# A decoder layer in fp32 on one core: value transposes one product later, and two empty steps a tile in the second batch's cross stage

## Chip, core and metric

One core of a Trainium2 chip runs the kernel. The metric is the device time of one execution in microseconds. The time before is the median of three runs.

## The reference

A decoder layer over two batches of 512 tokens with 1024 features. Three stages follow each other, each with a residual and a layer norm:

```python
x = _layernorm(x + attn(x, wq, wk, wv, wo))       # 32 query heads, 8 key/value heads of 128, causal window of 128
x = _layernorm(x + xattn(x, ctx))                 # round and clip x and ctx to 0..255, then one product 512x1024x1024 per batch
x = _layernorm(x + ffn(x, w_gate, w_up, w_down))  # 2752 inner features, silu(gate) * up, rounded to whole numbers
```

## The kernel before

TensorE (PE) does all products. Most of them are fp32 and go through Strassen's scheme (`strassen`, a generator): a pair of 128-row weight blocks times a 1024 x 512 right-hand matrix is done as seven products of four 128x128x256 matmuls, in the order 1, 6, 5, 2, 7, 4, 3, with sums on VectorE (DVE) and ScalarE (ACT) between them. Each product is one step of the generator (`yield`). The trace has two records for one fp32 matmul.

**Attention.** A group is one batch and one key/value head; there are 16. `pieces(m + 1)` yields the steps of the next group's projections while `scores` and `weigh` do the current group. `project` makes three Strassen runs for a group: j = 0 gives kT and vT, j = 1 and 2 give the queries. After the first run `transpose_v` turns vT into v by four PE transposes (tile `vtr`, L308), an ACT copy (L310) and a DVE difference `vd` (L312). A tile of 128 tokens has six calls of `other`, each of which takes one step of `pieces` and one step of work lent by `between`. The transposed probabilities `pt` (L374), the transposed values `vtr` and the weighted sums `o` (L395 to L398) all use the pool `ps_t`, which has one buffer.

**Output projection** (tiles `y`, L563, with left factors `ol` and right ones `or`, `ot`) runs as lent work behind the attention of batch 1 and the feed-forward of batch 0.

**Cross stage.** `Cross.tokens` handles the four tiles of a batch in the order 2, 3, 0, 1, so that tile 1 (t = 5 in the second batch) is the last. For each it yields steps: layer norm of x (two), quantise (DVE), `whole` (ACT, gives a1), eight PE transposes `q` (L679) with the ACT copy to a1T (L680), two halves of `m` (L686, eight bf16 matmuls each, read by DVE in L687 and L688), a second layer norm (L77 to L85, two steps), and eight transposes of x (L695) with ACT copies into x2T (L696).

**Feed-forward.** A unit is 128 gate and 128 up features of one batch: seven products with the right-hand matrix x2T (L132), `activate` (the ACT and DVE steps L786 to L798, giving `act`), and a part of the down product `d` (L818), which is done for two units at a time in batch 0. Batch 0 has 21 full units and a rest unit (`rest`, L810) of 64 + 64 features, then batch 1 follows. `load_down` loads the down weights, `split` and `rest_of_split` make their hi and lo parts (L767, L774). The products, `q`, `m`, the transposes of x and `rest` take PSUM buffers from one pool of two, `ps_p`; some products have a second pool.

**What sets the order.** The second batch's cross stage is lent work of batch 0's feed-forward. `in_feed_forward` is called once after each of the seven products of a unit, and the queue `aside` is

```python
aside.add(iter([None] * 28))
aside.add(cross.context(1), 2)
aside.add(cross_tokens(1), 2)
```

where the 2 means that a step is taken in every second call. Before the rest unit of batch 0, `finish_between()` issues all that is left in the queues. Then the right-hand differences of x2T[1] (L102) are made, which batch 1's products need. A scheduler below the kernel reorders independent instructions within each engine, taking the order of the source as the priority; tiles of a pool are given out in source order.

Of the kernel before, what the change touches and what calls it, by code (L numbers as in the profile page):

```python
# [118 lines left out]
def strassen(nc, spaces, work, left, right, outs, name, sums=None):  # L119

    c11, c12, c21, c22 = outs

    def like(y):
        return y if len(c11.shape) == 2 else y.rearrange("p (k c) -> p k c", c=c11.shape[2])

    def product(ps, k, start):  # L130
        for c in range(KH):
            nc.tensor.matmul(ps, left[k - 1][:, c, :], right[k - 1][:, c, :],  # L132
                             start=start and c == 0, stop=c == KH - 1, skip_group_check=True)

    def bank(k):
        return spaces[k // 2].tile([P, NH], F32, tag="p", name=f"prod{k}_{name}")

    if sums is None:
        sums = [work.tile([P, NH], F32, tag=f"st{k}", name=f"st{k}_{name}", bufs=1) for k in range(3)]
    p1, u2, u3 = sums  # L140
    one, two = bank(0), bank(1)
    product(one, 1, True)
    nc.scalar.copy(p1, one)
    yield
    product(two, 6, True)
    nc.vector.tensor_tensor(u2, two, p1, ALU.add)
    yield
    roomy = spaces[0] is not spaces[1]
    if roomy:
        three = bank(2)  # L150
        product(three, 5, True)
        yield
    product(one, 2, False)
    nc.scalar.copy(c11, like(one))  # L154
    yield
    product(two, 7, False)
    nc.vector.tensor_tensor(u3, two, p1, ALU.add)  # L157
    yield
    if roomy:
        nc.vector.tensor_tensor(c22, like(three), like(u3), ALU.add)  # L160
        four = bank(3)
        product(four, 4, True)
        nc.vector.tensor_tensor(c21, like(four), like(u3), ALU.add)
        yield
    else:
        three = bank(2)
        product(three, 5, True)
        nc.vector.tensor_tensor(c22, like(three), like(u3), ALU.add)
        yield
        product(two, 4, False)  # L170
        nc.vector.tensor_tensor(c21, like(two), like(p1), ALU.add)
        yield
    product(three, 3, False)
    nc.vector.tensor_tensor(c12, like(three), like(u2), ALU.add)
    yield
# [33 lines left out]
def attention(nc, tc, consts, xbuf, tpool, wpool, ps_p, ps_y, dram, kept, complete, between):  # L209
# [7 lines left out]
    with ExitStack() as ctx:  # L217
# [11 lines left out]
        PAIRS = 1 + G // 2  # L229
# [3 lines left out]
        def load_weight(n):  # L233
            if n >= len(order):
                return
            _, g, j = order[n]
            w = wpool.tile([P, 2, KC, P], F32, tag="w", name=f"w_{n}")
            for h in range(2):
                src = (wv_d if h else wk_d)[g] if j == 0 else wq_d[g * G + 2 * (j - 1) + h]
                nc.sync.dma_start(out=w[:, h], in_=src)  # L240
            weights[n] = w

        def prepare(n):
            if n < len(order):
                lefts[n] = strassen_left(nc, tc, wpool, weights[n], f"s_{n}")
# [20 lines left out]
        def project_first(outs):  # L266

            ps = [ps_p.tile([P, N], F32, tag="p", name=f"first{h}") for h in range(2)]
            for c in range(KC):

                for k, part in enumerate((ts(0, NH), ts(1, NH)) if c == 0 else (slice(None),)):
                    for h in range(2):
                        nc.tensor.matmul(  # L273
                            ps[h][:, part], weights[0][:, h, c], x0[:, c, part],
                            start=c == 0 and k == 0, stop=c == KC - 1, skip_group_check=True,
                        )
            for h in range(2):
                nc.scalar.copy(outs[h], ps[h])
            load_weight(2)
            prepare(1)  # L280
            right[0] = strassen_right(nc, tpool, x0, "t_0")

        def project(n):

            b, g, j = order[n]
            if j == 0:
                c1 = kT[b, g] = kvpool.tile([P, N], F32, tag="kT", name=f"kT_{n}")
                c2 = vT[b, g] = kvpool.tile([P, N], F32, tag="vT", name=f"vT_{n}", bufs=1)
            else:
                if j == 1:  # L290
                    qT[b, g] = qpool.tile([P, N // BLOCK, G, BLOCK], F32, tag="qT", name=f"qT_{b}_{g}")
                c1, c2 = (qT[b, g][:, :, 2 * j - 2 + h] for h in range(2))
            if n == 0:
                project_first((c1, c2))
                yield
                return
            outs = [c[:, ts(half, c.shape[1] // 2)] for c in (c1, c2) for half in range(2)]
            for k, _ in enumerate(strassen(nc, (ps_p, ps_y if b == 0 else ps_p), work, lefts.pop(n), right[b], outs, n)):
                if k == 4:
                    prepare(n + 1)  # L300
                elif k == 6:
                    load_weight(n + 2)
                yield LUMP if k == 4 else None

        def transpose_v(b, g):
            ps = ps_t.tile([P, TPB, P], F32, tag="t", name=f"vtr_{b}_{g}")
            for i in range(TPB):
                nc.tensor.transpose(ps[:, i, :], vT[b, g][:, ts(i, P)], ident)  # L308
            v[b, g] = kvpool.tile([P, TPB, P], F32, tag="v", name=f"v_{b}_{g}")
            nc.scalar.copy(v[b, g], ps)  # L310
            vd[b, g] = kvpool.tile([P, TPB - 1, P], F32, tag="vd", name=f"vd_{b}_{g}")
            nc.vector.tensor_tensor(vd[b, g], v[b, g][:, 1:], v[b, g][:, : TPB - 1], ALU.subtract)  # L312

        def pieces(m):

            b, g = groups[m]
            for j in range(PAIRS):
                yield from project(m * PAIRS + j)
                if j == 0:
                    transpose_v(b, g)  # L320
                    yield

        def scores(b, g, i, meanwhile):

# [106 lines left out]
        for _ in pieces(0):  # L431
            pass
# [150 lines left out]
class Cross:  # L583
# [74 lines left out]
    def tokens(self, b, x2T, complete):  # L658
        nc, a2, base = self.nc, self.a2[b], self.base[b]
        one, raw, work, ps_p = self.pools  # L660
        for i in (2, 3, 0, 1):
            while (b, i // 2) not in complete:
                yield
            t = b * TPB + i
            x = self.xres[t]
            yield from layer_norm(nc, work, x)
            yield
            tmp = raw.tile([P, D], F32, tag="raw", name=f"tmp_{t}")
            a1 = work.tile([P, D], BF16, tag="a1", name=f"a1_{t}", bufs=1)
            rows = work.tile([P, 1], F32, tag="rows", name=f"rows_{t}")  # L670
            self.quantise(x, 0, tmp)
            yield
            self.whole(a1, tmp, rows)
            yield
            nc.vector.tensor_tensor(rows, rows, self.c12[:, 1:2], ALU.mult)
            a1T = work.tile([P, KC, P], BF16, tag="a1T", name=f"a1T_{t}", bufs=1)
            ps = ps_p.tile([P, KC, P], BF16, tag="p", name=f"q_{t}")
            for c in range(KC):
                nc.tensor.transpose(ps[:, c, :], a1[:, ts(c, P)], self.ident_bf)  # L679
            nc.scalar.copy(a1T, ps)  # L680
            yield
            for e in range(2):
                half = ts(e, HALF)
                ps = ps_p.tile([P, HALF], F32, tag="p", name=f"m_{t}_{e}")
                for c in range(KC):
                    nc.tensor.matmul(ps, a1T[:, c, :], a2[c][:, half], start=c == 0, stop=c == KC - 1)  # L686
                nc.vector.scalar_tensor_tensor(tmp[:, half], ps, rows, base[:, half], ALU.add, ALU.add)  # L687
                nc.vector.scalar_tensor_tensor(x[:, half], tmp[:, half], self.s12, x[:, half], ALU.mult, ALU.add)  # L688
                yield
            yield from layer_norm(nc, work, x)  # L690
            yield
            for e in range(2):
                ps = ps_p.tile([P, KC // 2, P], F32, tag="p", name=f"x2_{t}_{e}")
                for c in range(KC // 2):
                    nc.tensor.transpose(ps[:, c, :], x[:, ts(e * (KC // 2) + c, P)], self.ident)  # L695
                nc.scalar.copy(x2T[:, ts(e, KC // 2), ts(i, P)], ps)  # L696
            if t in self.spill:
                nc.sync.dma_start(out=self.spill[t], in_=x)
            yield
# [524 lines left out]
```

## Time and profile before

| | |
|---|---|
| median of three runs | 1900.16 us (1898.99 to 1901.72) |
| profiled execution | 1899.1 us, span 1897.4 us |
| PE busy | 1870.3 us, 8666 records |
| DVE busy | 1370.6 us |
| ACT busy | 562.6 us |
| DMA | 416.88 MB, mean 220 GB/s |
| chain that ended last | PE 84%, DVE 10%, ACT 3%, DMA 2% |

PE, DVE and ACT are the matmul, vector and scalar engines, PEld is PE's weight load, SP issues DMAs. A row of the timeline has start (us), duration (us), engine, line, operation, out<-in and count; an idle time before it stands in brackets with what ended it. PE records overlap: one of 128x256 lasts 379 ns and the next starts 216 ns after it.

### The profile page before, as it was taken

To read this page: it belongs to the slowest core of one execution; us is meant where nothing else is said; L and a number is where in the kernel's file an instruction comes from. 1 tells how busy PE (TensorE), PEld (TensorE's weight loads), DVE (VectorE), ACT (ScalarE), POOL (GpSimd) and SP (SyncE) were. 2 spreads that over 40 slices of the span, in tenths; PEclk is the share of its full clock that TensorE was granted. 3 is DMA by queue.
4 is the path that set the end of the run, shared out by engine and by line. 5 is a ranking of instruction groups with operands and counts; after the bars stand their busy time and mean duration, and the time that the engine had idled before them with its cause. 6 is when DMAs were issued, how large, how long until landed. Compare 5 with 4: busy or idle time off the path is not lost.

```text
span 1897.4 us, 24656 instructions
## 1 busy us (share of the span) xinstructions
PE 1870.3 (99%) x8666; PEld 1548.1 (82%) x8678; DVE 1370.6 (72%) x3021; ACT 562.6 (30%) x1571; POOL 13.8 (1%) x32
## 2 busy tenths in 40 slices
PE   9999999999999999999999999999999999999997
PEld 6888888878888888888777888888788778888885
DVE  4678888787777676767787667767777697655657
ACT  1334433332211221233543111112233244321224
POOL 0000000000000000000000000000000000000000
PEclk9999999999999999999999999999999999999999
DMA  8478888777888888856368777766344244544431
GB/s 310 170 263 287 287 280 289 263 242 255 276 305 273 277 284 287 273 187 224 115 213 287 264 274 249 261 239 211 122 152 147 84 158 170 200 139 134 166 128 45
DMA packets 183323, 416.88 MB, mean 220 GB/s; under 512 B 16672, under 2 KB 93728, under 8 KB 183200
## 3 DMA queue, kind: packets, MB, share of 16 engines
q1 hardware_dynamic: 181760, 412.94, 63.5%
q10 hardware_dynamic: 1440, 2.36, 0.3%
q8 instruction: 69, 1.13, 0.2%
q14 instruction: 54, 0.44, 0.1%
HBM read 318.77 MB, written 96.47 MB: 219 GB/s over the span
## 4 chain that ended last, share of the span: by engine, by line
PE 84%; DVE 10%; ACT 3%; DMA 2%; issue 1%; SPq 0%; DVEq 0%; ACTq 0%
PE prod L132 49%; PE y L563 16%; PE d L818 7%; PE ps L338 3%; PE o L397 2%; PE o L398 2%; PE m L686 1%; PE pt L374 1%; DMA wd<-in_wd_dram 1%; PE first L273 1%; PE o L395 1%; ACT s L362 1%; DMA ol<-kept 1%; DVE factors L409 0%; DVE lo L774 0%
## 5 line engine op out<-in xcount | busy, mean ns | idle before, releaser
L563 PE MATMUL y<-or,ol 128*128 128x256 f32 x896 | 243.6, 379 | 1.3 <-DMA ol<-kept 1.2
L563 PEld LDWEIGHTS y<-or,ol 128*128 128x128 f32 x896 | 169.0, 190 | 28.0 <-issue 3.6
L563 PE MATMUL y<-ot,ol 128*128 128x256 f32 x672 | 184.3, 382 | 1.8 <-DVE ot L507 1.5
L132 PE MATMUL prod<-xT,w 128*128 128x256 f32 x752 | 182.7, 380 | 0.1
L132 PE MATMUL prod<-t,w 128*128 128x256 f32 x752 | 177.2, 379 | 0.0
L132 PE MATMUL prod<-t,s 128*128 128x256 f32 x752 | 176.7, 379 | 0.1
L132 PE MATMUL prod<-x2T,wgu 128*128 128x256 f32 x672 | 160.1, 380 | 0.2 <-DMA sgu<-sums 0.2
L132 PEld LDWEIGHTS prod<-t,w 128*128 128x128 f32 x752 | 140.1, 190 | 23.6 <-issue 6.7
L132 PE MATMUL prod<-t,wgu 128*128 128x256 f32 x672 | 159.4, 379 | 0.0
L132 PEld LDWEIGHTS prod<-xT,w 128*128 128x128 f32 x752 | 139.4, 190 | 24.3 <-issue 6.7
L132 PEld LDWEIGHTS prod<-t,s 128*128 128x128 f32 x752 | 140.3, 190 | 23.1 <-issue 4.8
L132 PE MATMUL prod<-t,sgu 128*128 128x256 f32 x672 | 155.7, 379 | 0.5 <-ACT g L154 0.5
L563 PEld LDWEIGHTS y<-ot,ol 128*128 128x128 f32 x672 | 124.8, 190 | 27.3 <-DVE ot L507 6.4
L132 PEld LDWEIGHTS prod<-x2T,wgu 128*128 128x128 f32 x672 | 127.3, 190 | 18.9 <-ACT g L154 0.6
L132 PEld LDWEIGHTS prod<-t,wgu 128*128 128x128 f32 x672 | 127.2, 190 | 18.9 <-issue 0.5
L132 PEld LDWEIGHTS prod<-t,sgu 128*128 128x128 f32 x672 | 127.2, 190 | 18.8 <-ACT g L154 0.9
L362 ACT ACTIVATE s<-s,top 128x128 f32<-128x128 f32 x256 | 99.6, 390 | 34.0 <-DVE top L359 33.2
L818 PE MATMUL d<-hi,act 128*128 128x512 f32 x256 | 108.6, 425 | 0.4 <-DVE act L798 0.2
L348 ACT COPY s<-ps 128x128 f32<-128x128 f32 x192 | 39.5, 232 | 228.1 <-PE ps L338 228.0
L832 DVE TENSOR_TENSOR acc<-d,acc 128x512 f32<-128x512 f32 x104 | 71.1, 690 | 43.5 <-PE d L818 43.1
L818 PE MATMUL d<-lo,act 128*128 128x512 f32 x256 | 101.1, 395 | 0.0
L157 DVE TENSOR_TENSOR st<-prod,st 128x256 f32<-128x256 f32 x89 | 37.5, 422 | 83.0 <-PE prod L132 82.7
(220 smaller groups left out, 2983.5 us busy)
## 6 DMA issues: line engine op xcount, KB each, us to landing
kept<-factors SPq DMA_DIRECT2D x112, 448.0 KB, 3.6
ol<-kept SPq DMA_DIRECT2D x112, 448.0 KB, 5.3
w<-in_wq_dram SPq DMA_DIRECT2D x64, 512.0 KB, 4.6
or<-wo_sums SPq DMA_DIRECT2D x64, 512.0 KB, 5.1
sgu<-sums SPq DMA_DIRECT2D x42, 768.0 KB, 6.4
or<-in_wo_dram SPq DMA_DIRECT2D x48, 512.0 KB, 4.6
wgu<-in_wgu_dram SPq DMA_DIRECT2D x42, 512.0 KB, 4.1
wd<-in_wd_dram SPq DMA_DIRECT2D x42, 512.0 KB, 3.5
```

Of the source, the lines that this page charges most:

```text
L132: nc.tensor.matmul(ps, left[k - 1][:, c, :], right[k - 1][:, c, :], start=start and c == 0, stop=c == KH - 1, skip_group_check=True)
L157: nc.vector.tensor_tensor(u3, two, p1, ALU.add)
L273: nc.tensor.matmul(ps[h][:, part], weights[0][:, h, c], x0[:, c, part], start=c == 0 and k == 0, stop=c == KC - 1, skip_group_check=True,)
L338: nc.tensor.matmul(ps[:, k, cut // BLOCK : G + 1].rearrange("p d w -> p (d w)"), qT[b, g][:, G * i + c].rearrange("p h w -> p (h w)"), kT[ ...
L348: nc.scalar.copy(s[:, c, c * BLOCK :], ps[:, k, : G - c].rearrange("p d w -> p (d w)"))
L362: nc.scalar.activation(s[:, h, :], s[:, h, :], AF.Exp, bias=top[:, h : h + 1], scale=QSCALE, accum_out=total[:, h : h + 1],)
L374: nc.tensor.transpose(ps[:, :, ts(c, BLOCK)], s[:, c, :], ident)
L397: nc.tensor.matmul(ps, v[b, g][:, i - 1, :], both, start=True, stop=False)
L398: nc.tensor.matmul(ps, vd[b, g][:, i - 1, :], cur, start=False, stop=True)
L563: nc.tensor.matmul(banks[bank][:, half], left[:, SLOT[j]], mine[j], start=grow[k][0] and g == 0 and half == 0, stop=g == LAST, skip_group_ ...
L818: nc.tensor.matmul(ps, act[:, ts(i, P)], half[:, part], start=start and k == 0, stop=stop and k == len(parts) - 1)
L832: nc.vector.tensor_tensor(acc[t][:, ts(e, HALF)], ps, acc[t][:, ts(e, HALF)], ALU.add)
```

## The change

In `pieces`, the transposes of a group's values are issued after the first product of the second Strassen run instead of before it. In `Cross.tokens`, for the second batch alone, a tile gets two steps in which nothing is issued: one after `whole`, and one after the copy to a1T.

```diff
@@ pieces
             for j in range(PAIRS):
-                yield from project(m * PAIRS + j)
-                if j == 0:
-                    transpose_v(b, g)
-                    yield
+                for k, lump in enumerate(project(m * PAIRS + j)):
+                    yield lump
+                    if j == 1 and k == 0:
+                        transpose_v(b, g)
+                        yield
@@ Cross.tokens
             self.whole(a1, tmp, rows)
             yield
+            if b:
+                yield
             nc.vector.tensor_tensor(rows, rows, self.c12[:, 1:2], ALU.mult)
...
             nc.scalar.copy(a1T, ps)
             yield
+            if b:
+                yield
             for e in range(2):
```

The line numbers of the profile before are those of the kernel before; in the changed kernel L308 to L312 stay, L374 is L375, L395 is L396, L679 is L682, L686 is L691, L695 is L700, and all that follows is five later.

## Prediction

> **What bounds the kernel now.** I read the page's shares first, then what PE itself waited for, then the timeline at the places that the edits touch. The page:
>
> ```profile
> PE 1870.3 (99%) x8666; PEld 1548.1 (82%) x8678; DVE 1370.6 (72%) x3021; ACT 562.6 (30%) x1571; POOL 13.8 (1%) x32
> ```
>
> PE works for 1870.3 of 1897.4 us. DVE is busy 72% and ACT 30%, so they set the end only where PE's next instruction needs something they have not finished. PE takes its instructions in one fixed order, so every stall of PE adds its full length. The built changed program holds the same number of instructions of every kind on PE, DVE and the DMA queues; ACT has two table loads fewer. What can move is the stalls alone. The list of what PE waited for (total us, times, longest us) has these three lines for the stages of the two edits:
>
> ```profile
> PE vtr L308 <- DVE vT L171: 1.3, 1, 1.3
> PE m L686 <- ACT a1T L680: 1.1, 1, 1.1
> PE m L686 <- DVE tmp L687: 1.0, 1, 1.0
> ```
>
> The whole prize is therefore 3.4 us: one wait of a value transposition, and two waits in second-batch tiles, at 1342.6 and 1388.6. The timeline at the second shows what such a wait is (start, us, engine, line):
>
> ```profile
> 1385.49 0.61 PE L679 MATMUL q<-ident_bf,a 128*128 128x128 bf16 x8
> 1385.94 1.51 PE L132 MATMUL prod<-t,wgu 128*128 128x256 f32 x6
> 1387.50 1.00 ACT L680 COPY a1T<-q 128x1024 bf16<-128x1024 bf16 x1
> 1388.56 1.90 PE L686 MATMUL m<-a,a1T 128*128 128x512 bf16 x7 [1.10 <-ACT a1T L680]
> ```
>
> Three instructions of a product (six records) stand between the transposes q and the matmul m, and ACT's copy of a1T ends later than they do.
>
> The last of the four tiles of the second batch, as it runs before the change:
>
> ```profile
> 1485.23 0.39 PE L679 MATMUL q<-ident_bf,a 128*128 128x128 bf16 x4
> ...
> 1493.28 1.89 PE L686 MATMUL m<-a,a1T 128*128 128x512 bf16 x7
> ...
> 1496.30 1.89 PE L686 MATMUL m<-a,a1T 128*128 128x512 bf16 x8
> ...
> 1498.23 0.75 DVE L687 SCALAR_TENSOR_TENSOR tmp<-m,rows,base 128x512 f32<-128x512 f32 x1 [0.22 <-PE m L686]
> ...
> 1500.02 0.68 DVE L77 BATCH_NORM_STATS2 ln_stats<-xres 128x6 f32<-128x512 f32 x1
> ...
> 1502.42 0.81 DVE L85 TENSOR_SCALAR xres<-xres,ln_mv,ln_r 128x1024 f32<-128x1024 f32 x1
> ...
> 1508.65 0.60 PE L695 MATMUL x<-ident,xres 128*128 128x128 f32 x4
> ```
>
> Between q, m and the transposes of x (L695) PE has 6.2 us and more of other products, so the whole chain q, a1T, m, layer norm costs nothing. The end of the first batch's units, after that tile:
>
> ```profile
> 1521.03 1.89 PE L132 MATMUL prod<-x2T,sgu 128*128 128x256 f32 x8
> 1522.75 6.17 PE L810 MATMUL rest<-x2T,wgu 128*128 128x512 f32 x14
> 1522.97 0.42 DVE L174 TENSOR_TENSOR g<-prod,st 128x256 f32<-128x256 f32 x1
> ...
> 1523.49 0.63 ACT L786 ACTIVATE sg<-g 128x512 f32<-128x512 f32 x1 [5.31 <-DVE g L174]
> ...
> 1528.76 1.89 PE L132 MATMUL prod<-x2T,wgu 128*128 128x256 f32 x8
> ```
>
> After unit 20's last product (ends at 1522.7) the activation of unit 20 is a chain of DVE and ACT steps, and PE meanwhile does the rest unit; no wait of PE stands in this stretch.
>
> **The change, part by part.** *The transposition of the values.* Steps eight and nine of a group trade places; the number of steps, the place of each loan of a step to other work, and every DMA issue stay. vtr now stands behind product 1 (eight records of 0.216 us spacing, 1.73 us: the prod rows above start 1.73 us apart for eight) and, in the built order, behind o instead of before it. The 1.3 us wait was for vT's last sum, queued on DVE behind sums of weights and kept factors (0.68 and 1.08 us each in the timeline at 404); 1.73 us covers it: -1.3. ACT's copy of v (0.585 us) and DVE's vd (0.55 us) come one product later; v and vd are for the next group, many products on. The single PSUM buffer that pt, o and vtr share is next asked for by the next tile's pt, several products behind, so 0 there; if that cover were gone it would be the 0.585 us copy, up to 15 times.
>
> *The empty steps, first three tiles.* In the built order 19, 48 and 14 PE instructions now stand between q and m of the first three tiles; 3 stood in the second one before, where the 1.1 us were lost: -1.1. The 1.0 us at 1342.6 is m's second half, which waits until DVE has read the first; DVE was at a 1.23 us split (L774). There the cover grows only from two instructions (0.86 us) to three (1.30 us). DVE's read is 0.2 + 0.75 us when DVE is free, so I take -1.0, and -0.4 if DVE is as late again.
>
> *The empty steps, last tile.* The cross stage's steps are called once in two products of the feed-forward, and the first batch has 21 units x 7 = 147 products. I counted the calls from the source: before, the four tiles start at calls 65, 85, 105, 125 and the last ends by call 147, exactly in time. With 12 steps a tile instead of 10 they start at 65, 89, 113, 137, and six of the last tile's twelve steps are left when the products end. finish_between then issues them all at once: second empty step, m, layer norm, x transposes. PE's order in the built program becomes: last product of unit 20, q x8, m x16, four d of unit 20, x transposes x8, rest, unit 22. Nothing else can be put between: rest (L810) takes its PSUM buffer from the same pool of two as q, m and the x transposes, after them; more d need act of the rest unit, or a bank that the first two hold; unit 22's products need x2T[1].
>
> I walk this by hand, with A = the end of unit 20's last product. q: A+0.45 (8 x 0.056). ACT stands with sg of unit 20 ahead of a1T: L174 A+0.2 to 0.62 (0.42; PE to DVE costs 0.2 in the rows above), sg to A+1.3 (0.63), a1T to A+2.25 (1.01, overlapping a little). m starts A+2.3: **stall 1.85**. m's sixteen end at A+5.75 (16 x 0.216). d needs act of unit 20. DVE's order there interleaves both chains: L787, L788, L789 (0.69, 0.69, 0.42) to A+3.2; ACT mag 0.63 to A+3.9; L795 0.43; L687 0.75, L796 0.69, L688 0.75, L797 0.69, L687 0.75, L798 0.69 to A+8.9, with 0.03 between. **Stall 3.15.** Four d take 0.95 to A+9.85. The x transposes need the layer norm: L688 to A+9.65, one bn_stats to A+10.4, then 3.2 us from the second bn_stats to the end of L85 (1500.02 to 1503.23 above): A+13.6. **Stall 3.8.** rest's buffer is free when ACT has copied the first x transposes (0.2 + 0.58 behind them): **stall 0.4**. Then rest covers the rest with 6.9 us (16 x 0.43): the second copy 0.58 and two right-hand differences 2.4 us. Behind rest, act of unit 21 now includes a table load for the sigmoid, which follows the tail's square root (1.28 us, as the ACT_TABLE_LOAD at 1501.75 in the timeline), and its d comes 9.5 us behind rest: about **0.5** more. Sum +9.7; I take ±2 for it, as DVE may run late by some queued 0.7 us steps or early by an overlap.
>
> Total: -1.3 -2.1 +9.7 = +6.3 us. The profiled execution took 1899.1 us (span 1897.4 and 1.7 around it); 1905.4 on that scale, and the median of the three runs is 1.1 us above it, so 1906.5. The scheduler's other small reorderings, whose like in the trace are gaps of 0.1 to 1.4 us, I take as ±2 with mean nothing.
>
> The clock: in this trace PE's last matmul starts at 1885.25. The busy times of two stretches behind it (the number before the DMA share, which is the last but one, is the mean granted clock) show full clock up to 1889 and about half of it after:
>
> ```profile
> 1885.00:1889.00 4.00, 0.53 (x5) 0.32 (x3) 4.00 (x17) 2.17 (x7) 0.00 (x0) 1.00 0.32 131
> 1889.00:1897.40 8.40, 0.00 (x0) 0.00 (x0) 3.63 (x14) 2.02 (x3) 0.00 (x0) 0.53 0.31 125
> ```
>
> The longest single stall of the walk is 3.8 us, just inside the 4 us that this row shows as harmless. I take no loss, and as the other end of the bound the half clock for one stretch as long as those 4 us, 2 us lost. [...]
>
> **The rivals.** *The tail is covered (faster).* If DVE and ACT had the last tile's chain done while PE still had other work, only the prize would remain: -3.4, 1896.7. It decides from 9.7 us of cover; the built order holds 0.95 us of d inside the chain and puts rest's 6.9 us behind it. Chance 0.05. *The tail is half as long (no change).* Here the two chains overlap better than I walked and PE waits 3 to 6 us: 1900 to 1903. For it: DVE rows overlap by up to 0.1 us each; against it: the chain is one of dependent steps on an engine in order. Chance 0.18. *The clock falls in the tail (slower still).* Stalls of 1.85, 3.15 and 3.8 within 13 us with 4.4 us of work between, then a half clock of 4 us or more: +2 to +4, 1908.5 to 1910.5. For it, the low density; against it, no single gap over 4 us. Chance 0.25. *The first edit does not do what it says:* the scheduler already moves vtr among products, so its 1.3 us may reappear at another group; 1 us either way inside the range.
>
> **How the numbers follow.** My forecast, +6.3 within 4.3 to 8.3, has 0.52. It gives 1906.5. Leaving out about a tenth at each end, the range reaches to the middle of the half-length tail and of the clock case: 1902.0 to 1910.5. About 0.2% (3.8 us) is what a measurement here can tell from nothing. Slower by more: forecast and clock case, 0.77. Within: 0.18. Faster: 0.05.
>
> **What would show it.** In the changed profile: the vtr wait and the two m waits gone; one stretch near 1520 where PE waits for a1T, for act and for xres (about 2, 3 and 4 us), with the x transposes directly ahead of rest; m and rest otherwise at their old durations. The prediction is wrong if that stretch shows under 4 us of PE idle time, if the clock in it is under 1, or if the attention stage changes by over 2 us.

## The result and the profile after

| | before | after |
|---|---|---|
| median on the same chip | 1900.41 us | 1912.40 us (1911.28 to 1914.61, six runs) |
| ratio to before, 95% interval | | 1.0064 [1.0055, 1.0074] |
| profiled execution | 1899.1 us, span 1897.4 us | 1912.1 us, span 1910.4 us |

The change makes the kernel 12 us slower. The forecast was 1906.5 us, with a range of 1902.0 to 1910.5: right in its direction, 6 us short in size, and the time lies 1.9 us above the range. In the profiled executions the difference is 13.0 us.

The first row of the page of the changed kernel. The engines do the same work as before; PE's busy time is 3.8 us longer (the trace has twelve PE records more, and a half clock makes some longer, see below); the other 9 us are idle time of PE:

```profile
PE 1874.1 (98%) x8678; PEld 1548.5 (81%) x8678; DVE 1371.1 (72%) x3021; ACT 560.8 (29%) x1569; POOL 13.7 (1%) x32
```

What PE waited for in the changed kernel (total us, times, longest us):

```profile
PE x L700 <- DVE xres L85: 3.0, 1, 3.0
PE d L823 <- DVE act L803: 2.7, 3, 2.3
PE o L398 <- ACT both L382: 2.2, 4, 1.5
...
PE m L691 <- ACT a1T L683: 1.7, 1, 1.7
...
PE vtr L308 <- ACT factors L402: 0.8, 4, 0.3
PE o L396 <- ACT cur L378: 0.7, 1, 0.7
```

The three waits of before on which the prediction rested are gone: vtr for vT (1.3), and m for a1T (1.1) and for tmp (1.0). The m line that is left is a new wait, in the last tile. In their place stand three long waits (x, d, m), which are the forecast tail, and small ones (o, vtr), which the sum did not have.

The tail in the timeline of the changed kernel (start, us, engine, line, with the idle time before it and its releaser in brackets):

```profile
1519.97 0.61 PE L682 MATMUL q<-ident_bf,a 128*128 128x128 bf16 x8
...
1520.69 0.63 ACT L791 ACTIVATE sg<-g 128x512 f32<-128x512 f32 x1 [5.30 <-DVE g L174]
1521.23 1.00 ACT L683 COPY a1T<-q 128x1024 bf16<-128x1024 bf16 x1
...
1522.28 3.63 PE L691 MATMUL m<-a,a1T 128*128 128x512 bf16 x16 [1.70 <-ACT a1T L683]
...
1528.19 0.50 PE L823 MATMUL d<-hi,act 128*128 128x512 f32 x1 [2.29 <-DVE act L803]
...
1532.40 1.97 PE L700 MATMUL x<-ident,xres 128*128 128x128 f32 x8 [3.01 <-DVE xres L85]
...
1534.19 8.34 PE L815 MATMUL rest<-x2T,wgu 128*128 128x512 f32 x16
...
1542.37 1.89 PE L132 MATMUL prod<-x2T,wgu 128*128 128x256 f32 x8
```

This is the order and the chain that the prediction walked by hand: q, wait, m, wait, d, wait, x, then rest. Two rows are longer than they should be. The eight x transposes start at 1532.40 and rest at 1534.19, 1.79 us for what takes 0.87 at full clock (before, eight of another tile from 1357.71 to 1358.58); the next product starts 8.18 us after rest, which takes 6.88 (sixteen times 0.43, as its last fourteen records before, from 1522.75 to 1528.76). The windows of the same stretch say why (the third number from the end of a row is the granted clock):

```profile
1523.00:1526.42 3.42, 2.90 (x14) 1.11 (x12) 2.72 (x6) 2.54 (x3) 0.00 (x0) 1.00 0.78 279
1526.42:1529.83 3.41, 1.20 (x4) 0.67 (x4) 3.41 (x6) 0.00 (x0) 0.00 (x0) 1.00 0.03 11
1529.83:1533.24 3.41, 0.84 (x4) 0.84 (x5) 2.04 (x8) 0.20 (x1) 0.00 (x0) 0.50 0.00 0
1533.24:1536.66 3.42, 3.42 (x9) 1.91 (x8) 2.45 (x2) 1.17 (x2) 0.00 (x0) 0.50 0.00 0
1536.66:1540.07 3.41, 3.41 (x9) 1.52 (x8) 1.23 (x1) 0.00 (x0) 0.00 (x0) 1.00 0.00 0
```

The clock fell to one half at 1529.83 and came back at 1536.66: it was at half for 6.83 us. The first number behind the comma is PE's busy time in the stretch.

To see where the time goes over the whole span, I compare the starts of the transposes of p (pt) with those of the same ones of before, at three places, and the end. Each number is one profiled execution, so differences under 1 us say little. The profiled execution of before was 1.3 us under its median, that of the first edit alone 1.2 us over its own.

| kernel | offset at 59 us | at 354 us | at 840 us | at the end of the span |
|---|---|---|---|---|
| after | -0.6 | 0.9 | 3.6 | 13.0 |
| first edit alone | 0.1 | 2.1 | 4.9 | 4.7 |
| second edit alone | -0.9 | -0.4 | -0.2 | 9.0 |

In these executions the first edit loses some 4 to 5 us little by little during attention (59 to 840 us), where a gain of 1.3 had been put; by the medians below it is 2.7. The second loses nothing there and 9 us at the end.

### The profile page after: what moved, and what is told of

Read it like the earlier page. It is cut to its first block, busy times and chain, and to the rows that moved or that the text cites. A ratio compares the mean times of both kernels' runs of the same rounds, so it can differ in the third digit from the quotient of the medians.

```text
span 1910.4 us, 24662 instructions
## 1 busy us (share of the span) xinstructions
PE 1874.1 (98%) x8678; PEld 1548.5 (81%) x8678; DVE 1371.1 (72%) x3021; ACT 560.8 (29%) x1569; POOL 13.7 (1%) x32
## 3 DMA queue, kind: packets, MB, share of 16 engines
q8 instruction: 69, 1.13, 0.2%
## 4 chain that ended last, share of the span: by engine, by line
PE 80%; DVE 12%; DMA 4%; ACT 3%; issue 1%; SPq 0%; DVEq 0%; ACTq 0%
PE prod L132 47%; PE y L564 14%; PE d L823 7%; PE ps L339 3%; PE o L398 2%; PE o L399 2%; DMA wd<-in_wd_dram 1%; PE pt L375 1%; PE m L691 1%; DMA sums<-sum 1%; PE first L273 1%; PE rest L815 1%; ACT s L363 1%; DVE lo L779 1%; DMA ol<-kept 1%
## 5 line engine op out<-in xcount | busy, mean ns | idle before, releaser
L791 ACT ACTIVATE sg<-g 128x512 f32<-128x512 f32 x43 | 27.1, 630 | 221.0 <-DVE g L174 220.8
```

What stands on the lines that cost most here:

```text
L791: nc.scalar.activation(a, g, AF.Sigmoid, scale=1.0 / 128.0)
```

## Experiments

The ratios are to the kernel before on the same chip, with their 95% intervals; 0.001 is 1.9 us.

### The two edits apart

Each edit alone, as in the diff above.

> Only the first edit: the values' transposes one product later, no empty steps. Theory A (the later place makes PE wait in the attention stage, because vtr now stands behind o and its PSUM buffer is free only when ACT has copied o; the drift of 3.6 us read at 800 us of the changed trace is this): 3 to 4 us slower than before, about 1904. Theory B (that drift is chance, from DMA arrivals of one execution): within 1 us of before. Theory C, as predicted: 1.3 us faster.

Measured: 1902.96 us, 1.0015 [1.0006, 1.0024].

> Only the second edit: the empty steps, with the transposes in their old place. Theory A: 2 us won in the first three tiles, 9.7 us lost at the end of batch 0's units, about 8 us slower than before, 1908 to 1909. Theory B: all of the 12 us is here, 1912.

Measured: 1909.24 us, 1.0046 [1.0033, 1.0058]. The two add up: 2.7 and 9.0 us against 12.0. So the second edit comes out near its forecast (its terms -2.1 and +9.7 make 7.6; the interval of the 9.0 reaches from 6.3 to 11.0 us), and the first edit has the wrong sign.

### The tail

In this one, both edits stay, and batch 0's rest unit takes its PSUM buffer from the other pool, so that it no longer has to stand behind q, m and x.

```diff
-            ps = ps_p.tile([P, N], F32, tag="p", name=f"rest_{u}")
+            ps = (ps_p if b else ps_y).tile([P, N], F32, tag="p", name=f"rest_{u}")
```

> The changed kernel, with the PSUM tile of batch 0's rest unit taken from the other pool, so that rest's matmuls need not stand behind the transposes of x: two of its eight now stand between q and m, six between m and d. Theory A (PE stalls at this place only because nothing else was allowed there, and the half clock follows from the stalls): 6 to 7 us less than the changed kernel, about 1906, stalls left of about 1.1 us at the x transposes and 1.5 us at unit 22, full clock throughout. Rival (the chain of DVE and ACT is itself the bound until unit 22 can start): rest only moves, and the time is within 2 us of the changed kernel.

Measured: 1905.20 us, 1.0028 [1.0019, 1.0037]. Seven of the twelve us go. What PE waits for in the tail, 1510 to 1560, and the clock there:

```profile
PE prod L132 <- ACT x2T L701: 1.1, 1, 1.1
PE x L700 <- DVE xres L85: 0.7, 1, 0.7
```

```profile
1528.00:1532.00 4.00, 4.00 (x12) 2.00 (x11) 3.56 (x10) 0.61 (x2) 0.00 (x0) 1.00 0.00 0
1532.00:1534.00 2.00, 1.32 (x11) 0.89 (x9) 1.03 (x3) 1.96 (x3) 0.00 (x0) 1.00 0.62 160
1534.00:1536.00 2.00, 0.87 (x6) 0.58 (x5) 1.25 (x2) 1.78 (x4) 0.00 (x0) 1.00 0.95 340
```

With rest's matmuls free to stand between q, m and x, most of the chain of left-over steps is covered, and the clock stays at 1.00 in this execution. The same buffer with the second edit alone:

> Both empty steps, the transposes of the values in their old place, and the rest unit's PSUM tile from the other pool. Theory A (the parts add): the run with both edits and that bank less the 2.8 us of the first edit, 1902 to 1903; by the parts read from the traces (2.1 us won in the tiles, some 3 us of stalls left at the end) 1 us slower than before. If the empty steps pay as a whole once the end is covered: faster than before by 0.5 to 1 us.

Measured: 1901.49 us, 1.0011 [1.0002, 1.0020]. Seven of nine us go here as well. The clock did not stay at 1.00 here: the profiled execution, which took 1905.94 us, 4.5 more than the median, has a half clock for 3.41 us. The longest gap of PE in the 15 us before it was 1.1 us:

```profile
1531.70:1535.11 3.41, 1.66 (x11) 1.37 (x12) 1.76 (x3) 3.23 (x5) 0.00 (x0) 1.00 0.90 291
1535.11:1538.52 3.41, 3.41 (x10) 2.69 (x9) 3.41 (x5) 0.68 (x2) 0.00 (x0) 0.50 0.04 17
```

The next keeps the first of the two empty steps only:

```diff
             self.whole(a1, tmp, rows)
             yield
+            if b:
+                yield
```

> The kernel before with the first of the two empty steps alone (after whole). The cross stage then has 44 steps instead of 48, and two instead of six are left when the products of batch 0 end: the end of the second layer norm and the transposes of x. Theory A (the loss goes with the length of the chain that is issued at once): only one stall, ahead of the x transposes, 1.5 to 3 us, at full clock; both m waits of the earlier tiles gone (2.1 us); within 1.5 us of before. Rival (any step left over at the end costs the whole layer norm chain and the half clock): 5 us slower or more.

Measured: 1906.75 us, 1.0041 [1.0028, 1.0053]. Four steps more instead of eight leave two over instead of six, the second half of the layer norm and the transposes of x, and still nearly the whole price is paid, as one stall of 5 us and a half clock that sets in within it:

```profile
1526.32 1.97 PE L697 MATMUL x<-ident,xres 128*128 128x128 f32 x8 [5.04 <-DVE xres L85]
```

```profile
1515.00:1520.00 5.00, 5.00 (x24) 3.62 (x24) 4.73 (x9) 1.05 (x1) 0.00 (x0) 1.00 0.23 79
1520.00:1525.00 5.00, 1.27 (x6) 0.77 (x5) 4.41 (x11) 2.38 (x4) 0.00 (x0) 0.84 0.85 274
1525.00:1530.00 5.00, 3.68 (x11) 2.43 (x12) 4.70 (x9) 2.17 (x4) 0.00 (x0) 0.50 0.32 123
```

The price does not scale with the number of steps left over. In this trace it is the distance from the layer norm to the x transposes that wait for it, and the half clock.

In the last of this row, one empty step in one tile, which the count of calls says still fits:

```diff
             nc.scalar.copy(a1T, ps)
             yield
+            if b and i == 3:
+                yield
```

> The kernel before with one empty step in one tile only: behind the transposes of a, in the last tile of the second batch. The 147 products of the first batch give just enough calls for it, so that no step is left over. Counting theory: the loss of the second edit is all in left-over steps. Then this has no stall in the tail, and the clock stays at 1.00 there: 1899 to 1901, and the 1.1 us wait of m for a1T stays or goes with the place of its tile. Rival: any empty step in the last tile makes the layer norm end too late, left over or not: stalls of 2 us and more in front of the transposes of x: 1902 to 1905.

Measured: 1900.01 us, 0.9999 [0.9990, 1.0007]. The x transposes stand ahead of unit 20's last products and wait for nothing; the only wait of PE between 1480 and 1545 is this one:

```profile
PE d L820 <- DVE act L800: 0.2, 1, 0.2
```

The counting theory holds: an empty step costs nothing until a step is left over. The wait of m for a1T (1.1) is gone, but a gain of that size can't be told from nothing here.

### The transposes: place, buffer, engine

The first edit alone, with the transposes one more product later (`k == 1`):

> As the run with the first edit alone, but with the transposes after the second product of the second Strassen run (two products later than before). Theory A (the wait is for ACT's copy of o, 0.58 us, which a further product of 1.73 us covers): the loss is gone, within 1 us of before. Rival (any later place reshuffles the scheduler's order and costs as much): 3 to 4 us slower than before.

Measured: 1904.06 us, 1.0018 [1.0009, 1.0027]: no better.

The transposes of batch 0 in a PSUM buffer of the other pool (the first edit alone otherwise):

```diff
-            ps = ps_t.tile([P, TPB, P], F32, tag="t", name=f"vtr_{b}_{g}")
+            ps = (ps_t.tile([P, TPB, P], F32, tag="t", name=f"vtr_{b}_{g}") if b else
+                  ps_y.tile([P, TPB, P], F32, tag="p", name=f"vtr_{b}_{g}"))
```

> The first edit alone, with vtr in the other PSUM pool in the first batch's eight groups, so that it need not wait for ACT's copy of o there. Theory V: 1 to 1.5 us less than the first edit alone, about 1901.5, and no wait of vtr in the first batch. Theory D: the waits of vtr go, but those of o for both and of y for ot stay, at most 0.8 us less than the first edit alone.

Measured: 1903.82 us, 1.0022 [1.0012, 1.0032]. vtr's waits for the buffer are gone in batch 0, but o's waits for `both` are 3.2 us in all, and nothing is won.

The kernel before, with only the difference vd (L312) issued one product later, the transposes and the copy where they were:

> The kernel before, with the transposes of the values and ACT's copy in their old place and only DVE's difference vd one product later. Theory D (the first edit costs time because vd, 0.55 us of DVE, now stands in DVE's queue ahead of sums that PE waits for soon, cur and both of the next tile and ot of the output projection): most of the loss of the first edit is here too, 2 to 3 us slower than before. Theory V (the loss comes from vtr itself, which waits on PE for ACT's copy of o behind four exponentials, and from the copy of v that is late in ACT's queue): within 1 us of before.

Measured: 1903.05 us, 1.0021 [1.0012, 1.0030]. That looked like the answer: vd's place in DVE's queue. The next two put vd on GpSimd, without and with the later transposes, to take it out of that queue:

```diff
-            nc.vector.tensor_tensor(vd[b, g], v[b, g][:, 1:], v[b, g][:, : TPB - 1], ALU.subtract)
+            nc.gpsimd.tensor_tensor(vd[b, g], v[b, g][:, 1:], v[b, g][:, : TPB - 1], ALU.subtract)
```

> The kernel before with vd on GpSimd, nothing moved: the control for the run with the later transposes. It takes 16 times 0.55 us off DVE, which waits often and is not the bound. Theory D: DVE's queue matters at the groups, so up to 2 us less than before, 1898 to 1900.5. Theory O: no change, 1900 +-1. Either is wrong if GpSimd is so slow with it that the next group's products wait for vd: then slower by the difference, up to 16 times.

Measured: 1907.91 us, 1.0036 [1.0024, 1.0049].

> The first edit alone, with the difference vd of the values computed by GpSimd instead of DVE; the empty steps are out. The first edit alone took 2.7 us more than before, vd alone one product later 3.3 us more. Theory D: it is vd's new place in DVE's queue that costs. With vd on another engine most of the loss goes: 1899 to 1901.5, within 1.5 us of before, and the landmarks of attention (the transposes of p) drift by less than 1.5 us between the first group and the last, where the first edit alone drifts by 4.8. Theory O: it is the transposes' new place on PE and ACT's later copy of v. Then vd's engine makes no difference: 1902 to 1904.

Measured: 1905.55 us, 1.0028 [1.0020, 1.0037]. And the one empty step together with GpSimd:

> Both together: one empty step in the last tile, vd on GpSimd. If the two are independent, the sum of their two differences from before; by theory D and the counting theory 1897 to 1900, the fastest of all. If GpSimd's difference is late for a product, it shows as a wait of PE for POOL and the time is above before.

Measured: 1905.92 us, 1.0027 [1.0016, 1.0037]. Both theories failed here: taking vd off DVE made things worse. Part of it is seen beside the vd at 160 us (the third group's attention, 156 to 203 us, which some expectations call the second group), in the run with vd on GpSimd and nothing moved:

```profile
160.43 1.00 POOL L312 TENSOR_TENSOR vd<-v 128x384 f32<-128x384 f32 x1 [25.13 <-ACT v L310]
...
160.82 0.64 DVE L359 TENSOR_SCALAR top<-top 128x4 f32<-128x4 f32 x1
```

DVE's step L359, on which the softmax waits, took 0.64 us instead of 0.16, and ended with GpSimd's. But these runs differ from before in more than vd: the built order has 226 other places on DVE and 114 on PE. The run with the difference alone moved has 154 and 61, while vd itself kept its index in DVE's queue in 8 of 16 groups and moved by one in six more (the expectation of a later run, below, counts 10 and four, and 271 other instructions, which the traces do not bear out). None of these runs had tested what I thought.

### Place and order apart

Why does a moved vd reorder others? `keep_in_program_order` ties an instruction behind the one issued last before it on its engine, in source order. The sums of the output weights (L1084) follow vd in the source, so that before they are tied behind vd; with vd moved they are tied behind whatever stands before it, the end of a softmax (L368). The scheduler then plans on from there.

Four kernels take the two apart. In three of them (all but the one in which nothing is moved) the order of PE, DVE, ACT and SP is that of before except for what is moved, held by a dependency of each instruction on the one ahead of it, which needs no semaphore; the ties are out.

```diff
-    tc.keep_in_program_order(nc.vector.tensor_tensor(s1, a21, a22, ALU.add))
+    (nc.vector.tensor_tensor(s1, a21, a22, ALU.add))
...
+    for engine, packed in ORDER.items():
...
+                tc.add_manual_dep(
+                    mine[at], before.name,
+                    mybir.DependencyInfo(mybir.DependencyClass.NoSync, mybir.DependencyReason.DATA), reason="keep_order",
+                )
```

Only vd later in DVE's queue:

> Only the 16 differences vd stand later in DVE's queue, at the index that they have with the first edit (1 to 13 instructions later); all else in the order of before. Theory D: vd's place in DVE's queue costs, as the run with the difference alone moved seemed to show (+3.3): 1902 to 1904. Theory T: 1900 +-1, because in that run vd kept its index in 10 of 16 groups and moved by 1 in four more, while 271 other DVE instructions changed place.

Measured: 1900.37 us, 1.0001 [0.9992, 1.0009]. vd's place costs nothing that can be told from noise (-1.5 to 1.7 us); theory D has fallen.

vd on GpSimd, in the order of before:

> vd on GpSimd, all else in the order of before. vd on GpSimd took 7.8 us more than before, with 226 places changed on DVE and 114 on PE. If the changed order made all of that: 1900 +-1.5. If GpSimd itself costs (its vd lasts 1.14 us, and DVE's 0.16 us step beside it lasted 0.64 us in the second group): 1903 to 1908. By theory T with an order's price like that of the moved difference (3.3) the rest is GpSimd's: about 1904.5.

Measured: 1903.44 us, 1.0019 [1.0010, 1.0027]. Of the 7.8 us that GpSimd seemed to cost, about 3.4 are its own, and the rest is then the other order; the two intervals just overlap.

Nothing moved, but vd passed over by the ties:

```diff
-            nc.vector.tensor_tensor(vd[b, g], v[b, g][:, 1:], v[b, g][:, : TPB - 1], ALU.subtract)
+            untied.add(nc.vector.tensor_tensor(vd[b, g], v[b, g][:, 1:], v[b, g][:, : TPB - 1], ALU.subtract).ins.name)
```

> Nothing is moved: source order, transposes, copy and difference as before. Only the ties differ: where an instruction is tied behind the one traced last on its engine, vd is passed over and the one before it taken. That changes 132 places on DVE, 59 on PE and 26 on ACT, nearly the same as with the difference alone moved (154, 61, 26). Theory T: as that run, +3.3, 1902 to 1904.5. Theories D and P: 1900 +-1.

Measured: 1902.58 us, 1.0014 [1.0005, 1.0023]. Nothing of the computation stands elsewhere in the source, and the kernel is 2.6 us slower. In the traces DVE's order here is nearly that of the run with the difference alone moved (1.0021): without the 16 vd, 30 of 3005 places differ. What happens to the sums is plain at 160 us. Before, the sums fill the time in which DVE has nothing to do but to wait for the exponentials (timeline of before):

```profile
160.44 0.16 DVE L359 TENSOR_SCALAR top<-top 128x4 f32<-128x4 f32 x1
160.52 0.42 DVE L1084 TENSOR_TENSOR wo_sum<-wo 128x256 f32<-128x256 f32 x1
...
163.51 0.69 DVE L368 TENSOR_TENSOR s<-s,inv 128x512 f32<-128x512 f32 x1
...
171.44 0.68 DVE L380 TENSOR_TENSOR cur<-pt,keep_cur 128x512 f32<-128x512 f32 x1
```

With the other tie they come behind the end of the softmax (timeline of the run with other ties; its lines are 16 further down):

```profile
160.35 0.16 DVE L375 TENSOR_SCALAR top<-top 128x4 f32<-128x4 f32 x1
162.49 0.42 DVE L162 TENSOR_TENSOR st<-prod,st 128x256 f32<-128x256 f32 x1 [1.97 <-PE prod L148]
...
163.03 0.69 DVE L384 TENSOR_TENSOR s<-s,inv 128x512 f32<-128x512 f32 x1
163.64 0.42 DVE L1100 TENSOR_TENSOR wo_sum<-wo 128x256 f32<-128x256 f32 x1
...
172.62 0.68 DVE L396 TENSOR_TENSOR cur<-pt,keep_cur 128x512 f32<-128x512 f32 x1
```

DVE stands idle for 1.97 us, the same sums come 3.1 us later and push `cur` from 171.44 to 172.62. In this group PE does not wait for it: its o stands 1.2 us later, behind more products. Between 50 and 860 us PE has these waits, 1.6 us in all, where before has one of 0.3 (o for `both`); vtr waits 1.3 us for vT in both:

```profile
PE o L413 <- ACT both L397: 0.7, 2, 0.4
PE prod L148 <- DVE qT L176: 0.6, 1, 0.6
PE y L579 <- DVE ot L523: 0.3, 1, 0.3
```

Which late sum makes which of these waits was not traced.

The transposes, the copy and vd later, everything else in the order of before (here the transposes are issued in the same step as product 1, so that no other step changes its place):

> The value transposes, their copy and their difference later, with every other instruction of PE, DVE, ACT and SP held in the order of before by dependencies that cost no wait. Only 33 places on DVE, 32 on ACT and 34 on PE differ; in the first edit alone 235, 89 and 135 differ. The first edit alone took 2.7 us more than before. Theory P (the new places of the moved instructions cost it): 1902 to 1904.5. Theory T (the loss comes from the other instructions, which the scheduler puts in another order because the instructions tied to program order are now tied behind something else): 1898 to 1901, and the 1.3 us wait of vtr for DVE is gone or smaller.

Measured: 1923.65 us, 1.0127 [1.0109, 1.0144], far outside of what either theory gave. In the timeline of this kernel at the same place:

```profile
162.78 0.57 ACT L403 COPY factors<-o 128x512 f32<-128x512 f32 x1
163.40 0.42 PEld L308 LDWEIGHTS vtr<-ident,vT 128*128 128x128 f32 x4 [2.19 <-ACT factors L403]
163.40 0.66 PE L308 MATMUL vtr<-ident,vT 128*128 128x128 f32 x4 [1.79 <-ACT factors L403]
```

The transposes now stand behind o and need the one buffer of `ps_t` that o has filled. ACT empties it only after four exponentials. In the first edit alone, ACT's copy comes at about the same time, but the scheduler has put ten records of a product ahead of the transposes, where the fixed order has four, and only 0.17 us are left:

```profile
162.35 0.56 ACT L402 COPY factors<-o 128x512 f32<-128x512 f32 x1
...
162.96 0.66 PE L308 MATMUL vtr<-ident,vT 128*128 128x128 f32 x4 [0.17 <-ACT factors L402]
```

So the later place is not free, and the new order keeps it cheap here. The 23.6 us are the price of one way to place the moved instructions among the others, not of every one. Only 3.9 us of them are waits of vtr for the buffer; PE waits more elsewhere too (ps for s 5.5, y for `ot` 5.4, prod for `st` 4.0 us), and how these follow from the fixed order was not traced.

Last, the first edit alone with ties that pass over the end of the softmax (L367, L368), so that the sums can go ahead of it again:

> The first edit alone, with ties that pass over the two DVE steps of the softmax's end (L367, L368 of before). In the run with other ties and nothing moved, the first sum of the output weights waited behind that end, DVE stood idle for 1.97 us at 160.5 of the second group, and cur came 1.2 us later; the built order of this kernel has the four sums ahead of it again, as before. Theory T: most of the first edit's loss (+2.7) goes: 1898.5 to 1901.5. Theory P (the transposes' place behind o is what costs, the one PSUM buffer included): as the first edit alone, 1902 to 1904.5. In between, near 1901.5: both.

Measured: 1903.31 us, 1.0018 [1.0009, 1.0027].

> The same, with one empty step behind the transposes of a in the last tile of the second batch, which alone changed nothing. By theory T 1898 to 1901.5, and without the waits of vtr for DVE (1.3) and of m for ACT (1.1) that before has, at best 2 us under before; by theory P 1902 to 1904.5.

Measured: 1902.18 us, 1.0014 [1.0005, 1.0023]. No gain: within the intervals, both are the first edit alone, which is what theory P expected. The traces still hint at the tie, in the first batch only (the last run has 0.4, 1.0 and 4.1 in the place of the second row):

| kernel | offset at 59 us | at 354 us | at 840 us |
|---|---|---|---|
| first edit alone | 0.1 | 2.1 | 4.9 |
| first edit, ties free | 0.1 | 0.7 | 4.3 |
| ties alone | -1.0 | 0.5 | 2.4 |
| vd later, fixed order | -1.0 | 0.0 | -0.2 |

Up to 354 us two thirds of the first edit's loss are gone with the ties free. Behind that it loses the same again, above all where the output projection's y waits for DVE's `ot` in the second batch: 2.0 us in three waits between 50 and 860 us, where the list of before has none. No version beat the kernel before.

## Why the prediction was wrong

Two of the three signs that it had named for being wrong came: the clock in the tail fell under 1 (0.50), and attention changed by over 2 us (4.2 between 59 and 840 us in the profiled execution). The third, under 4 us of idle time of PE in the tail, did not.

**The first edit, -1.3: the wrong sign.** Measured +2.7. Three steps of the working failed.

- *The prize.* The 1.3 us were there and went. But vtr had stood between pt and o in that group, and under its wait ACT's copy `cur` was finished. With vtr gone, o waits for `cur` itself: the 0.7 us of `PE o L396 <- ACT cur L378` after. Little more than half a microsecond was ever to be had.
- *The single buffer, "so 0 there".* I asked who wants the buffer after vtr, and not who holds it when vtr comes. Behind o, vtr waits for ACT to copy o out: four times up to 0.3 us after (0.8 in all), and up to 1.8 us where the order is not adapted.
- *"The scheduler's other small reorderings ... with mean nothing".* A tie to program order takes whatever stands before it in the source, so moving vd moved ties of other work, and that alone costs 2.6 us (1.0014) with nothing else changed. A mean of nothing is a poor guess where an edit moves such ties.

"vd comes one product later, 0" was right: in the order of before the later place of vd measures 1.0001. How the first edit's 2.7 us divide between the buffer and the ties is not settled, because the two don't add: the ties alone make 2.6, freeing them gives nothing back in the median, and holding the old order makes it 23.6.

**The first three tiles, -2.1: right in the waits that it named.** No wait of m for a1T or tmp is left between 1325 and 1515 in the changed kernel. Two smaller ones, of products, have come (0.3 and 0.2) and one of 0.6 of the x transposes for ACT's copy, so that 1.0 us is left of the gain by the waits:

```profile
PE x L700 <- ACT x2T L701: 0.6, 1, 0.6
PE prod L132 <- ACT a1T L683: 0.3, 1, 0.3
PE prod L132 <- DVE tmp L692: 0.2, 1, 0.2
```

**The last tile, +9.7: right in place and order; the sum is right by luck, since two errors cancel.** The steps left over, their order on PE and the three stalls are as walked. The stalls, counted as in the walk from the time at which the next matmul could have started (0.16 us more than in the brackets of the timeline), are 1.86, 2.45 and 3.18 us against 1.85, 3.15 and 3.8: DVE's interleaved steps overlap more than I allowed (each starts 0.08 to 0.09 us before the one ahead of it ends, between 1523.92 and 1528.80), which made the second stall 0.7 and the third 0.6 shorter. That is 7.5 instead of 8.8. The half clock adds 0.9 in the x transposes and 1.3 in rest, which makes 9.7 again; the 0.4 ahead of rest can't be seen apart from the slow x transposes, and of the 0.5 behind rest only a wait of 0.2 us (d for act) is there. The runs agree with the place: 1.0046 with the second edit alone, 0.9999 with the one step that fits.

**The clock: the wrong way round.** "I take no loss" is a further step that failed: the half clock cost 2.2 us. It was made a rival at 0.25, against which stood that no single gap lasted 4 us. When the clock fell, at 1529.83, no gap in the tail had been longer than 2.3 us, and a burst of 1.2 us had ended 0.4 us before. The row that I took as a limit showed a gap that was harmless once, not one that always is.

What the traces show of the falls is this. The half clock lasted 6.83 us in the changed kernel, with the second edit alone and with the first empty step alone, and 3.41 us with the second edit and the other pool. In the 3.41 us ahead of these four falls PE worked 1.20, 1.13, 1.25 and 1.66 us. Before, at the end of the kernel, the fall comes behind 3.41 us without work:

```profile
1886.10:1889.51 3.41, 0.00 (x0) 0.00 (x0) 3.38 (x15) 1.58 (x6) 0.00 (x0) 1.00 0.33 133
1889.51:1892.92 3.41, 0.00 (x0) 0.00 (x0) 2.83 (x12) 0.80 (x3) 0.00 (x0) 0.50 0.37 154
```

So the longest gap alone does not tell: before, the clock fell only 3.98 us after the end of PE's last matmul (1885.53), and with the second edit and the other pool it fell with no gap over 1.1 us ahead of it. Nor do the runs give a limit for the work: in the changed kernel PE worked 1.66 us in the 3.41 from 993.94 on and 1.12 in those from 1524.80 on, and the clock stayed at 1.00 in both. What sets off a fall was not shown.

**The sum.** With +2.7 in place of -1.3, the forecast of 1906.5 becomes 1910.5; the 1.9 us to the measured 1912.4 are within the intervals of the two edits' own runs. The rivals with a covered or a shorter tail were wrong. "1 us either way" for the first edit was the bound that was too narrow: its term was 4.0 us off, and with it right the range would have held the time.

## What to carry to other kernels

Before a step is moved in a kernel whose order is planned, list what is tied to it in program order, and compare the built orders with it moved and not moved: an experiment that moves one instruction tests that instruction only if the others stay. A buffer has two neighbours: ask who holds it when the moved step comes, not only who wants it next. Lent steps cost nothing until one is left over, so count the calls against the steps before adding any, and take a half clock into the sum as a risk where stalls of PE follow each other closely, even if no gap is long: in the changed kernel no gap of PE ahead of the fall was longer than 2.3 us, and the half clock cost 2.2 us.

## What was not expected of the hardware

In the tail the clock fell behind gaps of PE of at most 2.3 us in the changed kernel and of at most 1.1 us in the run with the second edit and the other pool, and some 2.1 us into a gap in the run with the first empty step alone. In the changed kernel it came back 4.3 us after PE had begun to work steadily (1532.40 to 1536.66).

In the run with vd on GpSimd and nothing moved, a step of DVE that takes 0.16 us before lasted 0.64 us at 160 us, beside a GpSimd subtraction of 1.00 us, and ended 0.03 us after it. The same subtraction took 0.55 us on DVE and 1.14 us on average on GpSimd, and moving 16 of them there cost 3.4 us (1.0019) with all else in order.
